# Moving VectorE's weight sums, two output sums and the index tables in a four-layer kernel

## The chip, the cores and the metric

The kernel runs on one core of one Trainium2 chip. The metric is the device time of one execution in microseconds (us). TensorE (PE) multiplies matrices, VectorE (DVE) and GpSimd (POOL) do elementwise work, ScalarE (ACT) does activations, and SyncE (SP) issues most of the transfers. Each engine takes its own instructions strictly in the order in which the program lists them; between engines, semaphores order the work.

## The reference, cut to what matters

Eight sequences of 128 tokens, 512 wide, in float32, pass four residual layers; each layer is a "cond" and an "ffn" part:

```python
x = x + L0_ffn(L0_cond(x))   # SwiGLU with per-sequence adapters; then a routed adapter layer
x = x + L1_ffn(L1_cond(x))   # adapters; routed adapters
x = x + L2_ffn(L2_cond(x))   # attention with a paged cache; soft routing
x = x + L3_ffn(L3_cond(x))   # routed adapters; 64 gated ranks

# L0_cond, per sequence b with adapter ids[b]:
g = x @ W_gate.T + adapter(x);  u = x @ W_up.T + adapter(x)      # 1376 wide
y = (silu(g) * u) @ W_down.T + adapter(...)

# L2_cond, 32 query heads on 8 key heads of 128, cache of 512 positions:
q, k, v = x @ Wq.T, x @ Wk.T, x @ Wv.T
q, k = rope(rmsnorm(q)), rope(rmsnorm(k))
k_all, v_all = [k_cache[block_table], k], [v_cache[block_table], v]
o = softmax(mask(q @ k_all.T / sqrt(128))) @ v_all
y = o @ Wo.T
```

The integer inputs are small tables: the adapter of each sequence for layers 0 and 1, its cache length, the pages of its cache and a language number for layer 3.

## The kernel before, in words

**Products with seven multiplications.** Projections, output products, gates and down products are computed as 2x2 blocks with seven block products in place of eight (Strassen, in Winograd's form). The left operand gives sums s1 to s4, the right one sums t1 to t4. `seven` (L956) writes one such product. Its PE order is: `one` = a11 b11; `p6` = s2 t2; `p5` = s1 t1; `six` = s3 t3; then a12 b21 onto `one`, s4 b22 onto `p5`, a22 t4 onto `six`. Two running sums u1 (L983: p6 plus `one`) and u2 (L985: p5 plus u1) are made by VectorE, and `six` plus u2 is written out (c22) before a22 t4 may be added onto the same bank; likewise u2 must have read `p5` before s4 b22 is added onto it. The argument `at` is a dictionary of hooks: whatever stands under "u1", "u2", "c22", "c12", "six" and so on is put into the program at that place.

**Attention in 32 steps.** A step n is a pair (qd, p): one of 8 key heads with its 4 query heads, and one of 4 pairs of sequences. I call the steps with p = 0, 1, 2, 3 the first to fourth of a head. In the loop of `run` (from L1307) step n does, in PE's order: scores of its first sequence (`weigh`, tile st, L1134), the projection q, k, v of step n + 1 (`project`: q_one, q_six, q_five, L970), the output product of step n - 1 (`leave`: wo_one, wo_two, wo_six, L970), scores of its second sequence, the first product with the values (`mix`, av, L1185), column sums (`summed`), the second product with the values.

VectorE's part of a step, in its order: four additions of the exponentials of the first sequence (`added`, part, L1154), the division of the output of step n - 1 (`divided`, oT, L1195, which waits for the reciprocals R that SP copies to other partitions), and then inside the projection's hooks u1, u2, the four left sums of the output product (`outputs`, os, L929), the blocks of q, k, v (L1019: first q and vals from `six`, then q and vals from `five`, then q and k from `six`), the rotation's straight products (r, L1064), the output product's u1 and u2, its block y (L1215), the rest of the rotation and its turn (qkt, L1111), the additions of the second sequence, the reciprocals of the sums (rr, L1170).

**The right sums of the weights** (`blocks.factors`, L877) are VectorE's too, four generators' steps per head: for the projection weights (tile q_s, 128x768 elements each) t1 and t2 are made at the end of a third step, t3 behind the first addition of the fourth step (L1313) and t4 in the hook "u2" of the projection there, behind the four left sums; for the output weights (tile o_s, 128x512 each) t1, t2 and t3 are made in the hook "c22" of the projection of a second step, and t4 in the hook "c22" of its output product. The first head's output weights are made in step 1, where the turn of a gathered cache block (kt, L1095) stands in the same hook.

**Shared order.** Once `running` is filled, nearly every instruction goes through `kept`, which holds it to the order of the program on its engine. POOL computes the rotation's crossed products (vq, vk, L1059) as soon as q and k are written, and issues the gathers of cached keys and values (L913).

**The start.** Layer 0's gates come in 11 slices of 128 columns (f = 0 to 10). Slice 0 is multiplied plainly; at its end the adapter products are masked by VectorE (tgm, tum, L369) and added. From slice 1 on `gates_by_seven` (L432) is used; per slice VectorE does u, p, p for each half of the tokens (L456, L457, L459) and, at the end, ten operations of L474 to L479. The loop (L541) also deals out the steps of the angle tables, three behind each slice from f = 2 on. Before that, the small integer tables are loaded by SP and turned into floats and row numbers by VectorE (`ints`, L130; mask1, kvrow L191, bias3): 3 casts, 1 mask, 2 x 11 operations for the cache rows and 2 for the bias. They have no fixed place in VectorE's queue; the scheduler put them between slice 0's operations.

```python
def some(ops, k=1):
    return lambda: [next(ops, None) for _ in range(k)]
...
    sums_of, outs = added(n, 0), iter(())
    next(sums_of)
    some(w_ops)()
    if n:
        divided(n - 1)
        outs = outputs(n - 1)
```

Of the kernel before, what the change touches and what calls it, by code (L numbers as in the profile page):

```python
# [10 lines left out]
F32 = mybir.dt.float32  # L11
I32 = mybir.dt.int32
AF = mybir.ActivationFunctionType
ALU = mybir.AluOpType
# [33 lines left out]
def forward(ctx: ExitStack, tc: tile.TileContext, a: dict, out: bass.AP):  # L48
# [81 lines left out]
    def ints(name, n, where=const):  # L130
        ti = where.tile([P, n], I32, tag=name + "_i", name=name + "_i")
        sp.dma_start(ti, a[name].partition_broadcast(P))
        tf = where.tile([P, n], F32, tag=name, name=name)
        dve.tensor_copy(tf, ti)
        return tf
# [27 lines left out]
        ALU.is_lt,  # L163
    )

    ids1 = ints("adapter_ids", NB)
    lens = ints("seqlens", NB)
    lang = ints("lang_ids", NB)
    table = ints("block_table", NB * 16, w0)


    mask1 = const.tile([P, NB], F32, tag="mask1", name="mask1")
    dve.tensor_scalar(mask1, ids1, p_div16, None, ALU.is_equal)

    kvrow = {}
    for what, order in (("v", "p (b c j) -> p b c j"), ("k", "p (b j c) -> p b c j")):
        selp = w0.tile([P, NB, 4, 4], F32, tag="selp", name="selp_" + what)
        dve.tensor_tensor(  # L180
            selp,
            table.rearrange(order, b=NB, c=4),
            block32.unsqueeze(1).unsqueeze(1).to_broadcast([P, NB, 4, 4]),
            ALU.mult,
        )
        page = const.tile([P, NB * 4], F32, tag="page", name="page_" + what)
        dve.tensor_reduce(page.rearrange("p (b c) -> p b c", c=4), selp, AX.X, ALU.add)
        dve.tensor_scalar(page, page, 32.0, p_mod32, ALU.mult, ALU.add)
        kvrow[what] = const.tile([P, NQ, NB * 4], I32, tag="kvrow_" + what, name="kvrow_" + what)
        for qd in range(NQ):  # L190
            dve.tensor_scalar(kvrow[what][:, qd, :], page, float(NQ), float(qd), ALU.mult, ALU.add)  # L191


    bias3 = const.tile([P, NB, 8], F32, tag="bias3", name="bias3")
    dve.tensor_tensor(
        bias3,
        eight.unsqueeze(1).to_broadcast([P, NB, 8]),
        lang.unsqueeze(2).to_broadcast([P, NB, 8]),
        ALU.is_equal,
    )  # L200
    dve.tensor_scalar(bias3, bias3, 5.0, None, ALU.mult)


    def load_small(dst_pool, name, shape, src, tag=None, bufs=None):
        kw = {} if bufs is None else {"bufs": bufs}
# [112 lines left out]
    with c0:  # L318
# [219 lines left out]
        banks = gates(0, first, lora_in)  # L538
        lora_gates(0, banks)
        rot, angles, turn_angles = rotary(tc, rp, w0, lens, part, rows, kept)  # L540
        for f in range(1, NF):  # L541
            after = f + 1 < NF and weight_sums(f + 1, gate_weights(f + 1))
            gates_by_seven(f, A)
            A = after
            if f == 2:
                down_loaded()
            for i in itertools.islice(angles, 3 * (f > 1)):
                kept(i)
            if f == NF // 2:
                AW = [down_weights(0, wop.tile([P, 3, NH, P], F32, tag="os", name="wds_0"))]  # L550
# [241 lines left out]
def attention(tc, a, x, ident, lens, kvrow, part, ww, wop, ypool, sums, rot, eps, psa, c2, chunks, mm):  # L792
# [106 lines left out]
    def every(ops):  # L899
        for _ in ops:  # L900
            pass
# [136 lines left out]
    def squares(n, m, j, heads):  # L1038

        for i in heads:  # L1040
            sq = wk.tile([P, HD], F32, tag="sq", name=f"sq{m}_{n}_{j}_{i}", bufs=1)
            col = i if m == "q" else REP
            kept(act.activation(sq, S[n][m][:, j, i, :], AF.Square, accum_out=S[n]["ssq"][:, j, col : col + 1]))  # L1043
# [104 lines left out]
    def added(n, j):  # L1148

        t, u = (wk.tile([P, REP * P], F32, tag=f"part{k}{j * (k == 0)}", name=f"part{k}_{n}_{j}", bufs=1) for k in range(2))  # L1150
        c = [S[n]["pT", j][:, k, :, :].rearrange("p i t -> p (i t)") for k in range(NC)]
        S[n]["part", j] = t
        for o, l, r in ((t, c[0], c[1]), (u, c[2], c[3]), (t, t, u), (t, t, c[4])):
            kept(dve.tensor_tensor(o, l, r, ALU.add))  # L1154
            yield
# [125 lines left out]
    def run(pool_, end_of, bank, keep):  # L1281
        late.append(pool_)
        y2 = ypool.tile([P, NB, D], F32, tag="y", name="y2")
        Y.append(y2)
        pool.memset(y2, 0.0)

        idle = psa.tile([P, 512], F32, tag="mm", name="idle_q", bufs=3)
        for _ in range(3):
            kept(pe.matmul(idle, x[:, 0, 0:P], x[:, 0, 0:512], start=True, stop=True))
        for j in range(2):  # L1290
            squares(1, "q", j, range(REP))
            squares(1, "k", j, (0,))
        keys_terms = rotate(1)
        read_cached = turn_cached(1, "xs")
        keys_terms()
        gather(1, "v")
        roots(1)
        rotated(1)
        normed(1)
        turn(1)  # L1300
        end, prepared = None, iter(())
        w_ops, wo_ops = iter(()), WO[0].factors()

        def some(ops, k=1):
            return lambda: [next(ops, None) for _ in range(k)]

        for n, (qd, p) in enumerate(steps):  # L1307

            after = n + 1 if 0 < n < len(steps) - 1 else None
            weigh(n, 0)  # L1310
            sums_of, outs = added(n, 0), iter(())
            next(sums_of)
            some(w_ops)()  # L1313
            if n:
                divided(n - 1)
                outs = outputs(n - 1)
                if not after:
                    every(outs)
            every(sums_of)
            if after:  # L1320
                project(after, {
                    "u2": lambda: (every(outs), every(w_ops)),
                    "c22": lambda: (turn_cached(2)() if n == 1 else None, some(wo_ops, 3)()),
                    "c11": lambda: (squares(after, "k", 0, (0,)), squares(after, "q", 0, (0, 1))),
                    "c12": lambda: squares(after, "q", 0, (2, 3)),
                })
                keys_terms = rotate(after)
                if n + 2 < len(steps):
                    if steps[n + 2][1] == 0:
                        weights(steps[n + 2][0])  # L1330
                    gather(n + 2, "k")
                leave(n - 1, {
                    "one": lambda: (
                        squares(after, "q", 1, range(REP)), squares(after, "k", 1, (0,)), roots(after),
                    ),
                    "c22": lambda: (every(wo_ops), keys_terms(), rotated(after), normed(after), turn(after)),
                })
                fetch(after)
                gather(after, "v")
            if n + 2 == len(steps):  # L1340
                end.load_w2()
                end.load_aw()
            mixed = mix(n, 0)
            left = (lambda: leave(n - 1),) if n and not after else ()
            weigh(n, 1, {2: (some(mixed), *left), 3: (some(mixed),), 4: (some(mixed, NC),)})
            if left:
                end.shifted()
            sums_of = added(n, 1)
            if n == 0:
                some(sums_of, 2)()  # L1350
                fetch(1, read_cached)
                gather(2, "k")
            every(sums_of)
            if 0 < n < len(steps) - 2 and steps[n + 2][1] == 0:
                w_ops = W[steps[n + 2][0]].factors()
                some(w_ops, 2)()
            summed(n)
            inverted(n)
            if n == 0:
                every(tokens(2))  # L1360
            if n == 5:
                prepared = end.prepare(bank, lambda shape, name: wk.tile(shape, F32, tag="xs", name=name, bufs=1))
            next(prepared, None)
            every(mix(n, 1))
            next(prepared, None)
            if n and p == 0:
                out_weights(qd)
                wo_ops = WO[qd].factors()
            if 0 < n < len(steps) - 2:
                turn_cached(n + 2)()  # L1370
                every(tokens(n + 2))
            if n == 3:
                kept(keep())
            if n == 4:
                end = end_of(kept)

            if qd == NQ - 1 and p:
                for j in range(2):
                    end.turn(y2, 2 * (p - 1) + j, bank)
            if n + 2 == len(steps):  # L1380
                end.low(0, bank)
                end.anchors(0, bank)
        divided(n)
        every(outputs(n))
        end.product(0, "st", bank)
        leave(n)
        return y2, end
# [903 lines left out]
```

## Time and profile before

| what | value |
|---|---|
| median of 3 runs | 1540.5 us (1537.6 to 1541.04) |
| the profiled execution's own time | 1540.52 us |
| its span from first to last instruction | 1538.6 us |
| granted clock of TensorE | 0.999 |
| PE busy in the span | 1510.6 us (98%) |
| DVE / POOL / ACT busy | 1048.7 / 843.9 / 543.9 us |
| PE busy from 345 to 1360 us (attention) | 1004.55 of 1015 us |
| PE busy from 0 to 170 us (gates) | 165.11 of 170 us |

A row of the timeline reads: start in us, duration in us, engine, line, operation, output<-inputs, shape, count, and in brackets the idle time of the engine just before it with what ended it. A row of the list of waits reads: who waited <- for whom: total us, how often, the longest. A row of the chain (the work that ended last, followed back) has start, duration and engine. Matmul rows come two to a float32 matmul, and their ends overlap the next row's start by some 0.16 us.

### The profile page before, as it was taken

To read this page: it belongs to the slowest core of one execution; us is meant where nothing else is said; L and a number is where in the kernel's file an instruction comes from. 1 tells how busy PE (TensorE), PEld (TensorE's weight loads), DVE (VectorE), ACT (ScalarE), POOL (GpSimd) and SP (SyncE) were. 2 spreads that over 40 slices of the span, in tenths; PEclk is the share of its full clock that TensorE was granted. 3 is DMA by queue.
4 is the path that set the end of the run, shared out by engine and by line. 5 is a ranking of instruction groups with operands and counts; after the bars stand their busy time and mean duration, and the time that the engine had idled before them with its cause. 6 is when DMAs were issued, how large, how long until landed. Compare 5 with 4: busy or idle time off the path is not lost.

```text
span 1538.6 us, 19053 instructions
## 1 busy us (share of the span) xinstructions
PE 1510.6 (98%) x6127; PEld 947.0 (62%) x6127; DVE 1048.7 (68%) x2057; ACT 543.9 (35%) x1336; POOL 843.9 (55%) x870
## 2 busy tenths in 40 slices
PE   9999999999999999999999999999999999999998
PEld 7888886444555555555555555555555556559886
DVE  4666435477877786777777677777867878755375
ACT  1111110144444444444444444445434445431110
POOL 2241105285766777676677767667777767531210
PEclk9999999999999999999999999999999999999999
DMA  7311001153655544564444445444445534332001
GB/s 234 115 42 31 1 0 62 53 146 96 176 146 151 142 110 123 141 175 115 127 143 117 123 136 171 117 128 144 122 123 141 166 110 127 101 111 92 1 9 50
DMA packets 157837, 169.92 MB, mean 110 GB/s; under 512 B 54272, under 2 KB 129216, under 8 KB 157600
## 3 DMA queue, kind: packets, MB, share of 16 engines
q1 hardware_dynamic: 139296, 131.27, 30.7%
q0 software_dynamic: 17056, 36.49, 8.0%
q8 instruction: 51, 0.84, 0.2%
q10 hardware_dynamic: 1376, 0.85, 0.2%
q14 instruction: 58, 0.48, 0.1%
HBM read 113.89 MB, written 42.07 MB: 101 GB/s over the span
## 4 chain that ended last, share of the span: by engine, by line
PE 88%; DVE 7%; DMA 3%; issue 1%; ACT 0%; POOL 0%; SPq 0%; ACTq 0%; DVEq 0%
PE st L1134 17%; PE av L1185 17%; PE g L362 8%; PE q_six L970 7%; PE wo_two L970 5%; PE dn L362 5%; PE q_five L970 4%; PE q_one L970 4%; PE wo_one L970 3%; PE wo_six L970 3%; PE eo_l L53 2%; PE h L1719 2%; PE z L1719 2%; PE o L1719 1%; PE midp_l L53 1%
## 5 line engine op out<-in xcount | busy, mean ns | idle before, releaser
L913 POOL DMA_INDIRECT kn<-in_k_cache,kvrow_k x256 | 279.8, 1093 | 73.3 <-issue 69.4
L913 POOL DMA_INDIRECT vals<-in_v_cache,kvrow_v x256 | 261.6, 1022 | 73.4 <-issue 62.6
L1185 PE MATMUL av<-pT,vals 128*128 128x512 f32 x640 | 298.8, 597 | 0.0
L1138 ACT ACTIVATE pT<-st,hide 128x512 f32<-128x512 f32 x256 | 175.9, 687 | 318.5 <-PE st L1134 194.4
L1134 PE MATMUL st<-qT,kT 128*128 128x512 f32 x512 | 236.4, 594 | 2.8 <-DMA qT<-turned_new 2.2
L1059 POOL TENSOR_TENSOR vq<-q,txq 128x256 f32<-128x256 f32 x128 | 120.3, 967 | 181.4 <-DVE q L1019 102.4
L1185 PEld LDWEIGHTS av<-pT,vals 128*128 128x128 f32 x640 | 118.9, 190 | 144.0 <-issue 142.1
L1134 PEld LDWEIGHTS st<-qT,kT 128*128 128x128 f32 x512 | 96.5, 190 | 112.9 <-issue 106.4
L1154 DVE TENSOR_TENSOR part<-pT 128x512 f32<-128x512 f32 x128 | 87.1, 687 | 64.7 <-issue 44.2
L1170 DVE RECIPROCAL rr<-sum 128x256 f32<-128x256 f32 x32 | 56.2, 1758 | 73.0 <-PE av L1185 37.8
L970 PE MATMUL q_one<-q,x 128*128 128x384 f32 x256 | 93.0, 486 | 0.0
L1043 ACT ACTIVATE sqq<-q 128x128 f32<-128x128 f32 x256 | 79.4, 310 | 22.9 <-DVE q L1019 15.9
L970 PEld LDWEIGHTS q_one<-q,x 128*128 128x128 f32 x256 | 48.5, 190 | 39.8 <-issue 14.4
L970 PE MATMUL q_six<-q_s,xs_all 128*128 128x384 f32 x192 | 69.8, 486 | 0.0
L1134 PE MATMUL st<-qT,kTn 128*128 128x512 f32 x128 | 65.5, 593 | 1.0 <-ACT pT L1138 1.0
L970 PE MATMUL wo_one<-o,oT 128*128 128x256 f32 x256 | 65.7, 379 | 0.0
L1024 ACT COPY q<-q_one 128x256 f32<-128x256 f32 x32 | 11.9, 372 | 145.9 <-PE q_one L970 145.9
L970 PE MATMUL wo_two<-o_s,os 128*128 128x256 f32 x256 | 60.8, 380 | 1.7 <-DVE vals L1019 1.3
L1138 ACT ACTIVATE pT<-st,rs 128x512 f32<-128x512 f32 x64 | 44.0, 687 | 38.3 <-PE av L1185 20.6
L970 PEld LDWEIGHTS wo_one<-o,oT 128*128 128x128 f32 x256 | 48.6, 190 | 13.4 <-PE st L1134 0.2
L429 POOL TENSOR_TENSOR ws<-wu 128x256 f32<-128x256 f32 (+1 forms) x9 | 6.4, 712 | 91.3 <-DMA wu<-in_WuT 82.4
L362 PE MATMUL g<-xs,ws 128*128 128x256 f32 (+1 forms) x240 | 55.1, 379 | 0.0
(450 smaller groups left out, 2796.5 us busy)
## 6 DMA issues: line engine op xcount, KB each, us to landing
turned_new<-qkt SPq DMA_DIRECT2D x126, 160.0 KB
turned_cached<-kt SPq DMA_DIRECT2D x128, 128.0 KB
kT<-turned_cached SPq DMA_DIRECT2D x32, 512.0 KB
qT<-turned_new SPq DMA_DIRECT2D x32, 512.0 KB
R<-R SPq DMA_DIRECT2D x96, 128.0 KB
q<-in_WqT SPq DMA_DIRECT2D x8, 1024.0 KB
o<-in_WoT SPq DMA_DIRECT2D x8, 1024.0 KB
kn<-in_k_cache,kvrow_k POOLq DMA_INDIRECT x256
```

What stands on the lines that cost most here:

```text
L53: pe.matmul(o, lhsT, rhs, start=start, stop=stop)
L362: pe.matmul(o, lhsT, rhs, start=start, stop=stop, skip_group_check=True)
L913: kept(pool.indirect_dma_start(out=d[:, c, :], out_offset=None, in_=kc if what == "k" else vc, in_offset=bass.IndirectOffsetOnAxis(ap=kvro ...
L970: kept(pe.matmul(o, l[:, c, :], r[:, c, :], start=start and c == 0, stop=c == 1, skip_group_check=True))
L1043: kept(act.activation(sq, S[n][m][:, j, i, :], AF.Square, accum_out=S[n]["ssq"][:, j, col : col + 1]))
L1059: kept(pool.tensor_tensor(to, t[:, b, :, hi : hi + 64], wx[:, b, lo : lo + 64].unsqueeze(2).to_broadcast(list(to.shape)), ALU.mult,))
L1134: kept(pe.matmul(ps, s["kT"][:, c, 4 * j : 4 * j + 4, :] if c < 4 else s["kn"][:, j], s["qT"][:, :, REP * j : REP * (j + 1), :].rearrange( ...
L1138: kept(act.activation(pT[:, c, :, :].rearrange("p i t -> p (i t)"), ps, AF.Exp, **(dict(bias=hide[:, b, c : c + 1]) if c < 4 else dict(bia ...
L1154: kept(dve.tensor_tensor(o, l, r, ALU.add))
L1170: kept(dve.reciprocal(r, S[n]["sum"]))
L1185: kept(pe.matmul(ps, v[:, c, :], pT[:, c, :, :].rearrange("p i t -> p (i t)"), start=c == 0, stop=c == NC - 1, skip_group_check=True,))
L1719: return pe.matmul(o, lhsT, rhs, start=start, stop=stop, skip_group_check=True)
```

## The change

Five things move; nothing is added to or removed from the work of the attention or the tables.

1. **Projection weights.** t3 and t4 of the next head's projection weights are both made at the start of the fourth step, ahead of the first addition. Before, t3 came behind that addition and t4 in the hook "u2".
2. **Output sums.** Two of the four left sums of the output product (os) go from behind u2 to between u1 and u2 of the projection (hook "u1"), in all steps 1 to 30.
3. **Output weights.** In a second step, t1 and t2 go from hook "c22" to hook "c12" of the projection, behind the q and vals of `five`; t3 goes to a hook "six" of the output product, which puts it behind the rotation's straight product and ahead of that product's u1; t4 stays.
4. **Step 1's turn of a cache block** goes along to hook "c12", behind t1 and t2.
5. **Tables.** The adapter, language and page tables are made by a generator; its 28 operations are dealt five to a slice of the gates behind the angle steps, from f = 3 on. Their three loads stand later in SP's queue, behind the norms' loads and ahead of the third slice's weights. The cache lengths stay where they were.

PE's, ACT's and POOL's instructions keep their order.

```diff
-    ids1 = ints("adapter_ids", NB)
     lens = ints("seqlens", NB)
-    lang = ints("lang_ids", NB)
-    table = ints("block_table", NB * 16, w0)
...
+    def tables():
+        read = {}
+        for name, n, where in (
+            ("adapter_ids", NB, const), ("lang_ids", NB, const), ("block_table", NB * 16, w0),
+        ):
+            ti = where.tile([P, n], I32, tag=name + "_i", name=name + "_i")
+            sp.dma_start(ti, a[name].partition_broadcast(P))
+            read[name] = ti, where.tile([P, n], F32, tag=name, name=name)
+        for ti, tf in read.values():
+            yield dve.tensor_copy(tf, ti)
...
+        yield dve.tensor_scalar(mask1, ids1, p_div16, None, ALU.is_equal)
...
         rot, angles, turn_angles = rotary(tc, rp, w0, lens, part, rows, kept)
+        tabled = tables()
         for f in range(1, NF):
...
-            for i in itertools.islice(angles, 3 * (f > 1)):
+            for i in itertools.chain(itertools.islice(angles, 3 * (f > 1)), itertools.islice(tabled, 5 * (f > 2))):
                 kept(i)
...
             sums_of, outs = added(n, 0), iter(())
+            if n:
+                some(w_ops, 2)()
             next(sums_of)
-            some(w_ops)()
             if n:
                 divided(n - 1)
                 outs = outputs(n - 1)
...
                 project(after, {
-                    "u2": lambda: (every(outs), every(w_ops)),
-                    "c22": lambda: (turn_cached(2)() if n == 1 else None, some(wo_ops, 3)()),
+                    "u1": some(outs, 2),
+                    "u2": lambda: every(outs),
                     "c11": lambda: (squares(after, "k", 0, (0,)), squares(after, "q", 0, (0, 1))),
-                    "c12": lambda: squares(after, "q", 0, (2, 3)),
+                    "c12": lambda: (
+                        squares(after, "q", 0, (2, 3)), some(wo_ops, 2)(), turn_cached(2)() if n == 1 else None,
+                    ),
                 })
...
+                    "six": some(wo_ops),
                     "c22": lambda: (every(wo_ops), keys_terms(), rotated(after), normed(after), turn(after)),
```

More of the change, by code (lines that the diff above doesn't have):

```diff
@@ L164, in forward @@
     )
-    ids1 = ints("adapter_ids", NB)
     lens = ints("seqlens", NB)
-    lang = ints("lang_ids", NB)
-    table = ints("block_table", NB * 16, w0)
     mask1 = const.tile([P, NB], F32, tag="mask1", name="mask1")
[L173 to L184, printed above, removed]
-        )
[L186 to L191, printed above, removed]
@@ L194, in forward @@
[L194 to L201, printed above, removed]
+    kvrow = {w: const.tile([P, NQ, NB * 4], I32, tag="kvrow_" + w, name="kvrow_" + w) for w in "vk"}
+    bias3 = const.tile([P, NB, 8], F32, tag="bias3", name="bias3")
+    def tables():
[8 more added lines that the diff above has]
+            yield dve.tensor_copy(tf, ti)
+        ids1, lang, table = (tf for _, tf in read.values())
+        yield dve.tensor_scalar(mask1, ids1, p_div16, None, ALU.is_equal)
+        for what, order in (("v", "p (b c j) -> p b c j"), ("k", "p (b j c) -> p b c j")):
+            selp = w0.tile([P, NB, 4, 4], F32, tag="selp", name="selp_" + what)
+            yield dve.tensor_tensor(
+                selp,
+                table.rearrange(order, b=NB, c=4),
+                block32.unsqueeze(1).unsqueeze(1).to_broadcast([P, NB, 4, 4]),
+                ALU.mult,
+            )
+            page = const.tile([P, NB * 4], F32, tag="page", name="page_" + what)
+            yield dve.tensor_reduce(page.rearrange("p (b c) -> p b c", c=4), selp, AX.X, ALU.add)
+            yield dve.tensor_scalar(page, page, 32.0, p_mod32, ALU.mult, ALU.add)
+            for qd in range(NQ):
+                yield dve.tensor_scalar(kvrow[what][:, qd, :], page, float(NQ), float(qd), ALU.mult, ALU.add)
+        yield dve.tensor_tensor(
+            bias3,
+            eight.unsqueeze(1).to_broadcast([P, NB, 8]),
+            lang.unsqueeze(2).to_broadcast([P, NB, 8]),
+            ALU.is_equal,
+        )
+        yield dve.tensor_scalar(bias3, bias3, 5.0, None, ALU.mult)
```

## The prediction, made blind

> **What bounds the kernel now.** I read the page's totals, then PE's waits, then the chain, then the timelines of single steps.
>
> ```profile
> PE 1510.6 (98%) x6127; PEld 947.0 (62%) x6127; DVE 1048.7 (68%) x2057; ACT 543.9 (35%) x1336; POOL 843.9 (55%) x870
> ```
> ```profile
> PE q_six L970 <- DVE vals L1019: 5.3, 10, 0.8
> PE st L1134 <- DMA qT<-turned_new: 2.2, 3, 1.6
> PE gu L362 <- DVE tgm L369: 1.8, 1, 1.8
> ...
> PE g L362 <- DVE p L457: 1.2, 2, 0.9
> ```
>
> PE is the bound: 1510.6 of 1538.63 us. PE's own work does not change, so the change can only move its gaps, 20.8 us in sum with 7.3 us of tail. The list says which are DVE's. To see what the list rounds away I measured, in every attention step, the stretch from the projection's first q_one to the next step's first st. The shortest, in step 8, is 590.09 to 605.16 = 15.07 us; the excess over it sums to 0.7 us in the first steps of the heads, 4.2 in the second, 4.5 in the third and 5.45 in the fourth. Below, a "place" is the time after the step's first q_one.
>
> **Fourth steps: a gain.** Step 15 starts its projection at 824.22.
>
> ```profile
> 822.57 0.69 DVE L1154 TENSOR_TENSOR part<-pT 128x512 f32<-128x512 f32 x1 [2.12 <-issue]
> ...
> 831.37 0.95 DVE L877 TENSOR_TENSOR q_s<-q,q_s 128x768 f32<-128x768 f32 x1
> 832.24 0.42 DVE L1019 TENSOR_TENSOR q<-q_six,uq 128x256 f32<-128x256 f32 x1
> 832.58 0.28 DVE L1019 TENSOR_TENSOR vals<-q_six,uq 128x128 f32<-128x128 f32 x1
> ```
> ```profile
> 832.91 0.91 PE L970 MATMUL q_six<-q_s,x 128*128 128x384 f32 x2 [0.79 <-DVE vals L1019]
> ```
>
> t4 (0.95, a pitch of 0.87) stands ahead of the q and vals that PE waits for, and the gap is 0.79: without it vals is in time. DVE idles 2.12 us before the first addition; t3 and t4 (0.87 each) fit there. Five of the seven fourth steps have about 1.9 to 2.15 idle there; steps 3 and 27 have only 0.43, so t4 delays their additions by some 1.3, but t3 leaves the additions' far side and the 1.5 us that u2 waits for q_five (829.44) takes most of it up. I take the whole excess: **-5.45**. Ends: -5.75 (the matmul overlap, 0.16, regained in two steps more) and 0 (PE's signals are late and vals was not what came last).
>
> **Third and first steps.** u2 needs u1's result, so the pitch between them is 0.65 for an instruction of 0.55 (step 2: u1 at place 4.60, u2 at 5.25); two os between them fill the 0.1 that is lost there and again behind u2. So u2 ends 1.8 behind u1's start in place of 1.2, and the q and vals that PE waits for end 3.0 behind it in place of 3.2. PE's s4 b22 (due at 6.45) now waits for u2 where u1 starts after place 4.6, hardly in step 2 and by 1.0 to 1.2 in steps 6 and 18, whose u1 comes at 5.6 and 5.8; these were late by about as much through vals before. Recomputed for each of the eight third steps, their excess goes from 4.5 to 3.04: **-1.4**; first steps, with the same 0.2: **-0.6** of 0.7. Ends together +1 (every later u2 counts in full) and -3 (0.2 earlier vals in all).
>
> **Second steps: a loss.** Step 9 starts its projection at 623.10.
>
> ```profile
> 630.09 0.68 DVE L877 TENSOR_TENSOR o_s<-o 128x512 f32<-128x512 f32 x1
> 630.80 0.69 DVE L877 TENSOR_TENSOR o_s<-o,o_s 128x512 f32<-128x512 f32 x1
> 631.41 0.69 DVE L877 TENSOR_TENSOR o_s<-o 128x512 f32<-128x512 f32 x1
> 632.02 0.42 DVE L1019 TENSOR_TENSOR q<-q_five,uq 128x256 f32<-128x256 f32 x1
> ...
> 633.08 1.35 DVE L1064 TENSOR_TENSOR r<-q,tsq 128x1024 f32<-128x1024 f32 x1
> ```
> ```profile
> 634.72 1.03 PE L970 MATMUL wo_six<-o_s,os 128*128 128x256 f32 x4
> ```
> ```profile
> 632.61 3.77 POOL L1059 TENSOR_TENSOR vq<-q,txq 128x256 f32<-128x256 f32 x4 [6.30 <-DVE q L1019]
> ```
>
> Before, three sums fill the time from place 6.99 (630.09) in which DVE would wait for q_five (final at 7.90, when PE's s4 b22 ends), and wo_six starts at 11.62 (634.72) without waiting. After, DVE idles from 6.99 to 7.94, and t1 to t3 come behind: q and vals 7.94 to 8.5, t1 to 9.16, t2, the two writes from `six`, r, then t3. With DVE alone, pitches 0.54 + 0.68 + 0.61 + 0.53 + 1.2 + 0.7 put t3's end near 12.3, 0.7 past 11.62. But POOL's four vq start 0.17 behind q (632.44 to 632.61), so at about 8.53, just when t1 runs, and they slow DVE's instructions that read SBUF twice, and are slowed:
>
> ```profile
> 868.27 1.77 DVE L1064 TENSOR_TENSOR r<-q,tsq 128x1024 f32<-128x1024 f32 x1
> ```
> ```profile
> 308.81 1.24 DVE L1064 TENSOR_TENSOR r<-q,tsq 128x1024 f32<-128x1024 f32 x1
> 309.98 0.94 DVE L1064 TENSOR_TENSOR r<-k,tsk 128x256 f32<-128x256 f32 x1
> ```
>
> The same r takes 1.24 or 1.77, and the small one 0.94 here against 0.41 at 871.52 with POOL idle; o_s rows range from 0.68 to 1.0. DVE and POOL seem to take turns, instruction by instruction. Dealt so, with 0.6 for a vq by itself (3.77 for four, less r's 1.26 in step 8): t1 to 9.16, vq to 9.75, t2 to 10.30, vq to 10.89, r to 11.97, vq to 12.56, t3 to 13.11. Then wo_six starts at 13.17 in place of 11.62: 1.6 late. The displacement also makes wo_two (s2 t2, due 9.89) 0.4 to 0.5 late, which is within that 1.6. Five ordinary second steps at 1.65 make 8.25; step 13 has 1.8 and step 5 1.97 (both start late), and step 1 about 3.6, because the cached block's two transposes (0.71 + 0.66) stand between t2 and the rest. Sum 15.6 against 4.2: **+11.5**. Ends: +4.5 (no turns: 0.8 in each, 2.6 in step 1) and +20 (POOL's first vq beats t1: wo_six at 14.4, 2.8 each).
>
> [...]
>
> **The copies of q.** Two of the three waits of st for DMA qT, 0.30 and 0.23 shown, follow second steps (9 and 25). There DVE's t4 and rest come 0.6 earlier relative to PE's later stream, so the copies start earlier: **-1.07** (each gap, some 0.25 of lost overlap and pickup included). Ends 0 and -1.1.
>
> **The head of the kernel.**
>
> ```profile
> 8.03 13.26 DMA adapter_ids_i<-in_adapter_ids
> ```
> ```profile
> 90.34 1.10 PE L362 MATMUL g<-x,ws 128*128 128x256 f32 x4 [0.89 <-DVE p L457]
> ```
>
> The tables land at 21.28, and DVE converts them until tgm at 26.43, which needs none of them (its masks come from another table) and only stands behind them; PE gets tgm's product at 26.90 after 1.83 of idling. After, tgm can run near 23.6, when PE's adapter product t is done (23.15), and PE goes from its former gu row to it at 25.08. Gain 26.90 - 25.08 and the overlap: **-2.05**. Ends: 0 (the cache lengths, whose table stays ahead, land later than now) and -2.1.
>
> The 28 operations return in slices 4 to 8, in front of the next slice's u, p, p. They take 0.63, 0.85, 0.44, 0.98 and 0.44 us there. Slices 5 and 7 wait for p already (0.89 at 90.34, 0.28 at 117.59), so all of theirs counts, 0.85 + 0.98; slice 4 has 0.52 of slack (+0.19), 6 has 0.44 (+0.05), 8 has 0.85 (0). **+2.07**; ends +0.5 (half of it runs while DVE waits anyway) and +3.3 (all of it). POOL's and SP's queues: the three loads pass behind two norm loads and ahead of slice 2's weights, 85 us before the first gather needs a row; nothing.
>
> **Sum.** -5.45 - 1.44 - 0.6 - 1.07 - 2.05 + 2.07 + 11.5 = **+3.0 us**, on 1540.52 of the profiled execution, which is the median (1540.5): 1543.5 us. 0.2% is 3.1 us, about what a measurement of this kernel can tell from no change.
>
> **Rivals.**
> - *A* (0.50), the forecast: t1 gets ahead of vq and turns are taken. 1543.5, with 1540 to 1547 by the single terms; half of it over +3.1.
> - *B* (0.25): POOL comes first, in half or all of the second steps. For it: q is written 0.05 before t1 can start, and in the row 868.27 0.03 of lateness was enough. Second steps +16 to +20: 1548 to 1552.
> - *C* (0.20), the other side: no turns. [...] It decides from a t3 that ends before place 12.9, where the second steps' loss equals the other gains (8.5). For it: POOL has been asleep for 6.3 us before vq, and o_s rows of 0.68 are the most frequent.
> - *D* (0.05): the change does not do what it says. vals is not what PE waited for in fourth steps, and the 5.45 stay: 1549.
>
> **How the numbers follow.** Slower by over 0.2%: 0.26 of A, B, D: 0.56. Faster: nearly all of C and a little of A: 0.19. The rest 0.25. The range from C's middle to B's nearer half: 1536.5 to 1550.
>
> **What would show it.** Right: in fourth steps no gap of q_six by vals; in second steps wo_six waiting for o_s some 1.5 us, vq rows of four over 4.2 us, o_s rows near 1.2; PE's gap by tgm gone from 26 us; slices 5 and 7 waiting 0.8 to 1 us more. Wrong: wo_six at place 11.6 to 12.4 (C), at 14 and later (B), or fourth steps still 15.8 us long (D).

## The result, and the profile after

The changed kernel took 1551.82 us in the median of 17 runs (1547.63 to 1556.99), the kernel before 1540.5 us (17 runs, 1535.37 to 1549.35): a ratio of 1.0065, 95% interval 1.005 to 1.0081, so 8 to 12 us slower. The forecast was 1543.5 us with a range to 1550. The profiled execution had a span of 1553.3 us against 1538.6 (+14.7), and that is split below.

First the page's line of busy times and the waits of PE, after:

```profile
PE 1516.9 (98%) x6127; PEld 952.8 (61%) x6127; DVE 1049.7 (68%) x2057; ACT 544.7 (35%) x1336; POOL 848.9 (55%) x870
```
```profile
PE wo_six L979 <- DVE o_s L886: 8.4, 8, 2.6
PE g L370 <- DVE p L465: 6.9, 2, 5.3
PE st L1143 <- ACT pT L1147: 4.4, 1, 4.4
PE wo_two L979 <- DVE o_s L886: 3.1, 8, 0.4
```

Two things are to be seen. q_six no longer waits for vals (5.3 us before), and wo_six and wo_two now wait for the output weights in all eight second steps, as forecast. But PE's busy time has grown by 6.3 us with the same 6127 rows, and there is a single wait of 5.3 us among the gates. Both were not forecast.

The busy time first. The windows over the gates (us from the start, then width, PE busy, PEld, DVE, ACT, POOL, and after them the granted clock):

```profile
92.00:94.00 2.00, 0.72 (x2) 0.66 (x3) 1.85 (x5) 0.00 (x0) 0.31 (x1) 0.64 0.00 0
94.00:96.00 2.00, 2.00 (x7) 1.55 (x6) 0.85 (x2) 0.00 (x0) 0.00 (x0) 0.50 0.00 0
96.00:98.00 2.00, 2.00 (x6) 1.64 (x5) 0.00 (x0) 0.00 (x0) 0.00 (x0) 0.50 0.00 0
```

From 92.56 on PE's clock was granted at half for 6.83 us. It was so again for 6.83 us at 358.8 and for 3.41 us at 379.3; before, it was so only in the last microseconds (from 1534.45).

Now the wait of 5.3 us. VectorE, GpSimd and PE in slice 5, after:

```profile
87.84 0.27 DVE L198 TENSOR_REDUCE page_v<-selp_v 128x32 f32<-128x128 f32 x1
88.15 1.20 DVE L199 TENSOR_SCALAR page_v<-page_v,within 128x32 f32<-128x32 f32 x1
89.38 2.97 DVE L201 TENSOR_SCALAR kvrow_v<-page_v 128x32 int32<-128x32 f32 x3
```
```profile
87.72 1.59 POOL L528 TENSOR_TENSOR wds<-wds,wd 128x640 f32<-128x640 f32 x1
89.27 1.53 POOL L528 TENSOR_TENSOR wd<-wd 128x640 f32<-128x640 f32 x1
90.76 1.55 POOL L528 TENSOR_TENSOR wds<-wd,wds 128x640 f32<-128x640 f32 x1
```
```profile
93.28 2.04 PE L370 MATMUL g<-x,ws 128*128 128x256 f32 x4 [5.30 <-DVE p L465]
```

The five table operations of slice 5 end at 92.35, 4.5 us after they began. The reduction takes its 0.27 us. page_v ends at 89.35, right behind a sum of GpSimd (89.31), and the last kvrow at 92.35, right behind another (92.31). One by one the three kvrow take 1.45, 0.17 and 1.51 us, about a microsecond each in the mean, for 32 elements. At the kernel's start, before the change, page_v took 0.24 and eight kvrow 0.78:

```profile
23.90 0.24 DVE L188 TENSOR_SCALAR page_v<-page_v,within 128x32 f32<-128x32 f32 x1
24.33 0.78 DVE L191 TENSOR_SCALAR kvrow_v<-page_v 128x32 int32<-128x32 f32 x8
```

The difference is GpSimd, which is forming the sums of the down weights just then (1.53 to 1.98 us each) and had no row between 20 and 27 us before the change; the run sums_later below tests that. PE waits for the p that stands behind them.

And a second step, step 9 of after (its projection starts at 637.88):

```profile
645.82 0.42 DVE L1028 TENSOR_TENSOR q<-q_five,uq 128x256 f32<-128x256 f32 x1 [1.82 <-PE q_five L979]
...
646.36 0.68 DVE L886 TENSOR_TENSOR o_s<-o 128x512 f32<-128x512 f32 x1
647.07 1.10 DVE L886 TENSOR_TENSOR o_s<-o,o_s 128x512 f32<-128x512 f32 x1
...
649.76 1.21 DVE L886 TENSOR_TENSOR o_s<-o 128x512 f32<-128x512 f32 x1
```
```profile
646.41 5.15 POOL L1068 TENSOR_TENSOR vq<-q,txq 128x256 f32<-128x256 f32 x4 [5.36 <-ACT sqq L1052]
```
```profile
651.12 1.10 PE L979 MATMUL wo_six<-o_s,os 128*128 128x256 f32 x4 [0.84 <-DVE o_s L886]
```

The three o_s rows are t1, t2 and t3. t1 starts 0.05 ahead of the first vq and takes 0.68; t2 takes 1.10 and t3 1.21; four vq take 5.15 where they took 3.77. wo_six starts at place 13.24 (forecast 13.17, before 11.62).

The whole difference of the two profiled spans, in us, by stretches that have the same work, with the prediction's term:

| stretch | before | after | difference | forecast |
|---|---|---|---|---|
| start to the first gate product of sums (first row g<-xs,ws) | 28.95 | 27.21 | -1.74 | -2.05 |
| from there to the first row of the adapter's down product (td) | 141.26 | 150.45 | +9.19 | +2.07 |
| down products, adapters, first projection | 138.28 | 138.28 | 0 | 0 |
| projection of step 1 to that of the next (first scores of step 1) | 42.76 | 47.21 | +4.45 | 0 |
| second steps' excess over 15.07 | 4.16 | 18.60 | +14.44 | +11.5 |
| fourth steps' excess | 5.45 | 0.00 | -5.45 | -5.45 |
| third steps' excess | 4.48 | 0.84 | -3.64 | -1.4 |
| first steps' excess | 0.68 | 0.38 | -0.30 | -0.6 |
| rest of attention, by subtraction (forecast: copies of q) | | | -0.63 | -1.07 |
| from the last projection to the end | 212.26 | 210.61 | -1.65 | 0 |
| sum | | | +14.67 | +3.0 |

### The profile page after: what moved, and what is told of

It reads as the page before. It is cut to its first block, busy times and chain, and to the rows that moved or that the text cites. A ratio compares the mean times of both kernels' runs of the same rounds, so it can differ in the third digit from the quotient of the medians.

```text
span 1553.3 us, 19053 instructions
## 1 busy us (share of the span) xinstructions
PE 1516.9 (98%) x6127; PEld 952.8 (61%) x6127; DVE 1049.7 (68%) x2057; ACT 544.7 (35%) x1336; POOL 848.9 (55%) x870
## 4 chain that ended last, share of the span: by engine, by line
PE 90%; DVE 6%; issue 1%; another core or an unknown queue 1%; ACT 0%; POOL 0%; DMA 0%; SPq 0%; DVEq 0%; ACTq 0%
PE st L1143 17%; PE av L1194 17%; PE g L370 8%; PE q_six L979 7%; PE q_five L979 5%; PE q_one L979 5%; PE dn L370 5%; PE wo_two L979 4%; PE wo_six L979 4%; PE wo_one L979 3%; PE eo_l L53 2%; PE h L1732 2%; PE z L1732 2%; DVE o_s L886 1%; PE o L1732 1%
## 5 line engine op out<-in xcount | busy, mean ns | idle before, releaser
L1068 POOL TENSOR_TENSOR vq<-q,txq 128x256 f32<-128x256 f32 x128 | 130.2, 1047 | 186.1 <-ACT sqq L1052 134.4
L1147 ACT ACTIVATE pT<-st,rs 128x512 f32<-128x512 f32 x64 | 44.0, 687 | 40.0 <-PE av L1194 20.6
L979 PEld LDWEIGHTS wo_two<-o_s,os 128*128 128x128 f32 x256 | 47.9, 190 | 12.2 <-PE wo_one L979 6.1
```

The source lines that it names most:

```text
L979: kept(pe.matmul(o, l[:, c, :], r[:, c, :], start=start and c == 0, stop=c == 1, skip_group_check=True))
L1068: kept(pool.tensor_tensor(to, t[:, b, :, hi : hi + 64], wx[:, b, lo : lo + 64].unsqueeze(2).to_broadcast(list(to.shape)), ALU.mult,))
L1147: kept(act.activation(pT[:, c, :, :].rearrange("p i t -> p (i t)"), ps, AF.Exp, **(dict(bias=hide[:, b, c : c + 1]) if c < 4 else dict(bia ...
```

## The experiments

Times of one set are compared on one chip, with runs of the kernel before beside them. "Excess" is, as in the prediction, what a step needs over 15.07 us from its first q_one to the next st.

### First set: the parts taken apart

**tables_back**: the changed kernel, its tables as before.

```diff
+    ids1 = ints("adapter_ids", NB)
     lens = ints("seqlens", NB)
+    lang = ints("lang_ids", NB)
+    table = ints("block_table", NB * 16, w0)
...
-            for i in itertools.chain(itertools.islice(angles, 3 * (f > 1)), itertools.islice(tabled, 5 * (f > 2))):
+            for i in itertools.islice(angles, 3 * (f > 1)):
```

> The changed kernel with the tables loaded and converted at the start, as before; the weight sums and output sums stay moved. Theory 1 (of the 12.8 us between the two profiled executions, some 7.4 arise ahead of attention: three row operations of VectorE each wait for a weight sum of GpSimd of 1.5 us, TensorE idles 5.3 us and then runs 6.8 us at half its clock): the first q_one of attention comes near 299 us as before, no halved clock in the gates, and the time is 7 us under the changed kernel, about 5 us (0.35%) over the kernel before. Theory 2 (the tables cost the 2 us that the prediction took, the 5.3 us were a chance of that one execution): about 10 us (0.65%) over the kernel before, and a halved clock shows up elsewhere.

Measured: 1539.35 against 1532.15 us, ratio 1.0058 (1.0041 to 1.0075), so +9 us by the ratio. The gates' stretch is 140.91 us, with no halved clock there. The halved clock and the 5.3 us belong to the tables, as theory 1 has it. The time is above its +5 all the same. That number was taken off the 12.8 us between two profiled executions, and the one of before had a high excess in its attention (14.8 us; 9.1 in tables_only, which has the same order there); this may be the reason, but no run of before was profiled on this chip.

**outw_back**: the changed kernel, the output weights' sums and step 1's turn of a cache block as before.

```diff
-                    "c12": lambda: (
-                        squares(after, "q", 0, (2, 3)), some(wo_ops, 2)(), turn_cached(2)() if n == 1 else None,
-                    ),
+                    "c22": lambda: (turn_cached(2)() if n == 1 else None, some(wo_ops, 3)()),
+                    "c12": lambda: squares(after, "q", 0, (2, 3)),
...
-                    "six": some(wo_ops),
```

> The changed kernel with the output weights' sums (and the cached block's turn in step 1) where they were before; tables, projection weights and output sums stay moved. Theory 1 (all the loss in attention is in the eight second steps, some 14 us plus the wait and halved clock of step 1): wo_six never waits for o_s, and the time is about 2 us under the kernel before (-0.1%, with the gates still 7.4 late and the third and fourth steps 10 us better). Theory 2 (the gains of the third and fourth steps come from the later place of the output weights, the loss from elsewhere): third and fourth steps lose again and the time is at or above that of the changed kernel, +10 us.

Measured: 1532.23 against 1532.15, ratio 0.9996 (0.998 to 1.0012). Second steps' excess 2.14 us, third 0.32, fourth 0; no wait for o_s. Theory 2 falls. Slice 5 waits 5.31 us here too, and 6.83 us at half the clock follow.

**both_back**: both of these, so that only the projection weights and the two output sums are moved.

> Only the projection weights and the two output sums are moved; tables and output weights as before. Theory 1 (parts add up): third, fourth and first steps lie at 15.07 us from q_one to st, second steps as before, and the time is 8 to 10 us under the kernel before (-0.6%). Theory 2 (what VectorE gains in fourth steps is given back in the second steps of the next head or in the copies of q): within 3 us of the kernel before.

Measured: 1523.55 against 1532.15, ratio 0.9956 (0.9939 to 0.9974): 4 to 9 us faster. Excess: second steps 1.65, third 1.41, first and fourth 0. Theory 1.

**tables_only**: the kernel before, with the tables alone dealt among the gates.

> The kernel before with the tables alone loaded later and dealt among the gates. [...] Theory 2 (the prediction: 2.05 us gained at tgm, 2.07 lost in slices): 0, within 1.5 us.

Measured: 1539.49 against 1532.15, ratio 1.0063 (1.0046 to 1.0081). Its gates' stretch is 148.79 us, slice 5 waits 5.32. Theory 2, the prediction's zero for the tables, is refuted.

### Second set: why the tables are slow

**after_again**: the changed kernel on the chip of this set.

> The changed kernel itself, beside the kernel before on the chip of this set. Theory 1 (parts add up: -8.6 for the weight and output sums, +8.7 for the tables, +15.8 for the output weights, each measured in the first set): about +14 to +16 us over the kernel before. Theory 2 (the second steps' delay and the late tables share a cost, so that the +10 of the result holds on any chip): +10.

Measured: 1552.5 against 1540.36, ratio 1.0084 (1.0059 to 1.0109): 9 to 17 us, which holds both theories' numbers. Inconclusive between them; that the kernel is slower by about 0.7% is repeated.

**sums_later**: outw_back with GpSimd's down sums at slice 9, where only the last three table operations stand.

```diff
-            if f == NF // 2:
+            if f == 9:
                 AW = [down_weights(0, ...)]
```

> Weight sums, output sums and tables moved as in the change, output weights as before, and GpSimd's four sums of the down weights at slice 9 in place of slice 5, where no table operation stands. Theory 1 (the row operations are slow because each waits for one of GpSimd's sums): kvrow rows take 0.1 us each, slice 5 waits 1.5 to 2 us in place of 5.3, the clock is not halved there, 5 to 7 us under the kernel before. Theory 2 (they are slow by themselves in that place): slice 5 still waits 5 us and the time is that of the kernel before.

Measured: 1532.53 against 1540.36, ratio 0.9955 (0.9935 to 0.9975). Slice 5 of this kernel:

```profile
87.06 0.35 DVE L201 TENSOR_SCALAR kvrow_v<-page_v 128x32 int32<-128x32 f32 x3
```
```profile
88.35 1.10 PE L370 MATMUL g<-x,ws 128*128 128x256 f32 x4 [0.52 <-DVE p L465]
```

The same three kvrow take 0.35 us, not 2.97, in the same place of VectorE's queue; PE waits 0.52 us, its clock stays whole, and the gates' stretch is 143.57 us. The operations are slow only beside GpSimd's sums. Even r_sin's last operation, ahead of them, takes 0.43; in slice 5 of before it was

```profile
87.76 1.65 DVE L1425 TENSOR_SCALAR r_sin<-r_sin 128x512 f32<-128x512 f32 x1
```

Of the 2.3 us by which this stretch is longer than in before (141.26), most is in slice 7, where PE waits 1.52 us (before 0.28), and in slice 9, where it waits 0.75: there one of the last table operations stands beside the moved sums and takes 1.42 us.

**warm**: outw_back with ten matmuls without use ahead of the product that waits in slice 5. They write into the unused half of the tile of `one`, and slice 5's gates are not the reference's.

```diff
                 into(one[:, 0], a12, b21, False)
+                if f == 5 and one is B[0][0]:
+                    for _ in range(10):
+                        kept(pe.matmul(one[:, 1], a12[:, 0, :], b21[:, 0, :], start=True, stop=True, ...))
                 into(two[:, 1], s4, b22, False)
```

> Weight sums, output sums and tables moved as in the change, output weights as before, and ten matmuls without use in slice 5, ahead of the product that waits (their result is not read). Theory 1 (the clock is halved because TensorE has idled 5.3 us): the gap shrinks to 1 us, no halved clock near 92 us, and with the same end of VectorE's work the time is 2 to 3 us under the same kernel without them, so 2 to 3 us under the kernel before. Theory 2 (the halving has another cause): the clock halves there all the same and the time is that of the kernel before.

Measured: 1537.24 against 1540.36, ratio 0.9984 (0.9969 to 0.9999). PE and the windows of this kernel:

```profile
93.30 1.10 PE L370 MATMUL g<-x,ws 128*128 128x256 f32 x4 [1.02 <-DVE p L465]
```
```profile
94.00:96.00 2.00, 2.00 (x11) 1.74 (x10) 0.86 (x3) 0.00 (x0) 0.00 (x0) 1.00 0.00 0
```

The product starts at 93.30, as in after (93.28), since VectorE is as late. But its four rows take 1.10 us and not 2.04, and the window from 94 to 96 is at full clock. The gates' stretch is 146.96 us against 150.08 in outw_back: 3.1 us were the clock, which was halved behind 5.31 us of idle time and stayed whole behind 1.02. The gain in time fits (some 2 us between the two ratios, on different chips), though the intervals alone would not show it.

**idle_tables**: tables late, dealt five to a slice, but into VectorE's idle time behind the last u, p, p of a slice; output weights as before.

```diff
                 B.append((one, two, six, p1, u, b21, b22, t4))
+            for i in between:
+                kept(i)
             for one, two, six, _, _, b21, b22, t4 in B:
```

> Weight sums and output sums moved, output weights as before, tables loaded late, but dealt five to a slice into VectorE's idle time, behind the last u, p, p of a slice and ahead of its end. Theory 1 (the tables cost only because they stand with GpSimd's sums in front of a waiting TensorE): no gap over 1 us at slices 5 and 7, no halved clock in the gates; 9 to 10.5 us under the kernel before. Theory 2 (any table operation dealt among the gates delays them): 3 to 5 us under it.

Measured: 1530.42 against 1540.36, ratio 0.9935 (0.9912 to 0.9958): 6 to 14 us faster than the kernel before, and 22 us faster than the changed kernel in the same set (which also has the output weights' move). Gates' stretch 141.40 us, as without any tables in it. Theory 1. The operations that were slow in after now come one slice earlier, in slice 4, where GpSimd forms no sums; in slice 5 five others stand beside the sums:

```profile
75.97 0.24 DVE L199 TENSOR_SCALAR page_v<-page_v,within 128x32 f32<-128x32 f32 x1
76.24 0.35 DVE L201 TENSOR_SCALAR kvrow_v<-page_v 128x32 int32<-128x32 f32 x3
```
```profile
90.50 2.07 DVE L201 TENSOR_SCALAR kvrow_v<-page_v 128x32 int32<-128x32 f32 x5
94.53 0.42 DVE L484 TENSOR_TENSOR up<-g,u 128x256 f32<-128x256 f32 x1 [1.96 <-PE g L370]
```

These five still wait for GpSimd (2.07 us), but VectorE is idle for 1.96 us behind them, so nothing waits for them. Whether the late tables make this kernel faster than both_back, whose tables stay at the start, the two intervals do not tell.

### Third set: the second steps, and each move alone

**no_cross**: tables_back with GpSimd's vq left out in second steps.

```diff
+            if after and p == 1:
+                S[after]["zero"] = zero = wk.tile([P, 2, REP, HD], F32, tag="vq", ...)
+                kept(pool.memset(zero, 0.0))
...
-            for b in (...):
+            for b in () if zero else (...):
```

> The changed kernel with the tables as before, and in second steps GpSimd's four crossed products of q (vq) left out: their place is filled with zeros before the projection, so these steps' q is not the reference's. [...] Theory 2 (the order of VectorE's queue alone makes the delay): o_s rows as with vq, 1.7 each, +7.

Measured: 1532.33 against 1531.42, ratio 0.9998 (0.9981 to 1.0014). The same step's t2 and its wo_six:

```profile
626.84 0.69 DVE L877 TENSOR_TENSOR o_s<-o,o_s 128x512 f32<-128x512 f32 x1
```
```profile
630.21 1.10 PE L970 MATMUL wo_six<-o_s,os 128*128 128x256 f32 x4 [0.56 <-DVE o_s L877]
```

t2 takes 0.69 and not 1.10, t3 0.94 (vk is still there), and an ordinary second step's excess is 1.02 in place of 1.70. So 0.7 of the 1.7 us is due to GpSimd's vq. The other 1.0 is the order of VectorE's queue together with vk, beside which t3 takes 0.25 more than t2. The turns with vq and the order of the queue (theory 2) each hold a part; which is the larger, this run leaves open.

**t3_early**: tables_back with t3 directly behind t1 and t2.

```diff
-                        squares(after, "q", 0, (2, 3)), some(wo_ops, 2)(), ...
+                        squares(after, "q", 0, (2, 3)), some(wo_ops, 3)(), ...
-                    "six": some(wo_ops),
```

> The changed kernel with the tables as before, and t3 of the output weights directly behind t1 and t2, ahead of the last q and k of the projection and of r. Theory 1 (PE waits for t3 because r and two vq stand before it): wo_six is 0.4 late through wo_two alone, but r, u1, u2, y and t4 come 0.6 later and the last wo_six waits for t4; the second steps' excess is 1.2 in place of 1.7, +3 to +4 us over the kernel before. Theory 2 (what counts is that three sums stand behind q_five's values at all): 1.7 as before, +7.

Measured: 1535.41 against 1531.42, ratio 1.0024 (1.0005 to 1.0043). By the time this is theory 1; by the trace it is nearly theory 2. An ordinary second step's excess is 1.56: wo_six no longer waits for t3, but in its place the next wo_two waits 0.36 for u2 of the output product, which comes later by the same sum. The delay moves along the queue and does not go; the order of before, with the sums ahead of q_five's values, where VectorE idles, had no such wait.

**proj_only** and **os_only**: the kernel before with one move each.

> The kernel before with the projection weights' t3 and t4 alone moved. By the prediction the fourth steps gain 5.45 and the others nothing: -5.5 us. If the two output sums carry part of the -8.6 that both gave together, this is -5 to -6 and the rest is theirs; if they carry nothing, -8.6.

> The kernel before with the two output sums alone moved. By the prediction third steps gain 1.4 and first steps 0.6: -2 us; in fourth steps t4 still stands ahead of vals, and their 5.5 us of waiting stay. If the sums' place is worth more than the prediction took, -3 to -4.

Measured against 1531.42 us: proj_only 1530.36, ratio 0.9991 (0.9973 to 1.001); os_only 1524.94, ratio 0.9953 (0.9935 to 0.9971). In the traces both have lost the fourth steps' excess: 0.08 and 0.95 us (before 5.45). So the two output sums, which I had given nothing in fourth steps, take PE's wait there away almost alone, although t4 still stands ahead of vals: two os less in that stretch are 0.7 us, and the gaps that fourth steps had were 0.54 to 0.79. The time of os_only, 4 to 10 us less, is beyond what I expected (-2, or -3 to -4). The time of proj_only does not show what its trace shows, which the last set was for.

### Fourth set: do the two moves overlap

> Projection weights alone moved, on one chip with the two kernels it is compared with. Theory 1 (in fourth steps either move alone takes vals off PE's way, since the gap was 0.44 to 0.79 us and each move gives 0.7 to 0.9, so the two overlap): -4 to -6 us against the kernel before. Theory 2 (the first set's -1.1 is right and this move is worth next to nothing): -2 to 0.

> The two output sums alone moved. Theory 1 (overlap): -6 to -7 us, most of what both give. Theory 2: -2, as the prediction took them, and -6.5 was a chance of the executions.

> Both moved. Theory 1 (overlap): -8 to -9, clearly less than -5 and -6.5 added. Theory 2 (parts add up): the sum of the two lone results of this set.

> Both and the output weights moved, tables as before: the output weights' own cost is the difference to the kernel with both. Theory 1 (eight second steps by 14 us, and a halved clock of 1.7 behind step 1 in most executions): +15 between the two. Theory 2 (as between the changed kernel and the one with the output weights put back): +10 to +12.

These are the kernels proj_only, os_only, both_back and tables_back again, on one chip. Measured against 1534.76 us:

| kernel | median | ratio (interval) | excess in the trace |
|---|---|---|---|
| projection weights alone | 1528.06 | 0.9939 (0.9919 to 0.9959) | 4.4 |
| two output sums alone | 1524.91 | 0.9927 (0.9906 to 0.9948) | 4.9 |
| both | 1526.56 | 0.9942 (0.9917 to 0.9967) | 4.0 |
| both, and output weights | 1537.34 | 1.002 (1.0001 to 1.0039) | 16.4 |

The three upper kernels cannot be told apart: within the intervals, each move alone gives what both give. By the ratios the single moves gave 9.4 and 11.2 us, which would add up to 20.6, and both gave 8.9 (5 to 13). So they overlap, more than theory 1 had it; theory 2 is refuted for proj_pair, os_pair and both_pair. The output weights cost 12.4 us in excess between the two lowest rows, and 11 to 12 us in time, nearer to theory 2's number; in the first set it was 15.8. I take 11 to 16 us for it. That proj_only gave -1.4 on its chip (interval -4.1 to +1.5) and -9.4 here (-12.4 to -6.3) is more than the intervals allow; what differs between the two chips no run here tells, so the first is left as it stands and the size of a single move is not known better than that.

## Why the prediction was wrong, step by step

**What failed: the gates' term, "+2.07; ends +0.5 and +3.3".** It measured +9.19 in the trace. The step that failed is "They take 0.63, 0.85, 0.44, 0.98 and 0.44 us there": these durations came from rows at the kernel's start, where GpSimd was not forming sums, and were carried into slices where it is. I let VectorE and GpSimd take turns in the second steps, with the right rows, and did not ask what GpSimd runs in slice 5. I also let the turns slow only operations that read SBUF twice; page_v and kvrow read one SBUF tensor and were slowed all the same (1.20 us for page_v, 2.97 for three kvrow; 0.24 and 0.35 in sums_later). r_sin's 1.65 us in slice 5 of before (0.43 without GpSimd), one source too, was the sign of both. Slice 5's operations took 4.5 us and not 0.85, 3.7 more than priced. On that came 3.1 us of halved clock, which no term had, because the trace of before shows no idle time of PE over 1.83 us there, and slice 7 waited 0.35 us more than its term. Together that is the 7.1 us between +2.07 and +9.19; with +9.19 in its place the prediction's sum would be +10.1, inside the measured 8 to 12. What is left to the 14.7 of the two profiles is about the first scores' 4.45; the errors of the other terms cancel. Without tables the gates' stretch was 140.9 to 141.3 us in the eleven profiled kernels that have none there; with them, as dealt in the change, 148.8 to 150.5 in four.

**The head: right in the trace, and partly luck.** -1.74 for -2.05. But the eleven kernels with the tables at the start reached the same point between 26.2 and 29.1 us, 27.8 in the mean, and the seven with late tables between 26.3 and 27.5, 27.1 in the mean. The profile of before was near the slow end, so the gain is more like 0.8 us.

**Second steps: right in mechanism, too small by 3.** An ordinary one cost 1.70 for 1.65, and turns are taken as worked out (rows above). The turns were my estimate from r's 1.24 and 1.77 us; the runs show t2 at 1.10 us beside vq and at 0.69 without it (no_cross). Step 1 was 6.31 and not 3.6. The 3.6 itself was sized right: tables_back, with the same wait of 2.57 us there and no halved clock, has 3.67. In after, the halved clock behind the first scores still ran for the first 2.5 us of this step, and another 3.41 us of it came with the wait, together some 2.9 us (after_again 5.70, outw_pair 4.20). And the 4.2 us of before that the new excess replaces were a high draw, which makes the measured difference smaller: with the output weights in their old place the eleven other executions had 1.6 to 3.8.

**Fourth steps: right as a sum (-5.45) and in what PE waited for; the other half was missed.** Rival D is refuted, vals was what PE waited for, and the projection weights' move alone takes the excess to 0.08 (proj_only). But os_only shows that the output sums alone nearly do it too (0.95), so in the change the first move adds little that can be measured. The size had luck in it: with the order of before, tables_only had 3.82 and not 5.45.

**Third and first steps:** -3.94 for -2.0, past the far end given (-3). With the order unchanged (tables_only) third steps' excess was 2.4 and not 4.5, so a part of it is chance.

**First scores of step 1: not forecast, and by the runs hardly the change's.** They waited 4.4 us in the profiled execution of after and 2.5 in that of after_again, the same kernel; 3.0 in both_back and 1.0 in both_pair, again one kernel; 0.5 to 2.5 in most others and not at all in four. In before and tables_only ACT started pT there about 2.1 us apart, each on a signal of PE; in after the first pT started 5 us behind its product and the next ones 0.7 us apart. I have not found what makes ACT late; it stays open.

**The rivals.** The time fell at rival B's, for another cause: in all eight second steps t1 starts ahead of the first vq (0.05 us in step 9). Rival C (no turns, which with the second steps' low end of +4.5 gives -4.0 us and 1536.5) is refuted by t2's 1.10 us. The rival I lacked was a second place for the mechanism of the first.

## What to carry to other kernels

An operation's duration belongs to its place: before it is moved, list what the other engines run there, and price it with rows from that place; here a VectorE operation of 32 elements took 0.1 us alone and 1 us beside GpSimd's sums. Where an engine has idle time in a step, put the moved work into that idle time: here the tables behind the last u, p, p of a slice cost the gates nothing, five of them beside GpSimd's sums, and at the slices' ends they cost 8 to 9.5 us, or 2.3 with the sums moved away from slice 5. And where two moves each remove one cause of the same wait, price them together: either alone gave, as far as could be measured, what both gave.

## What the runs showed of the hardware

**Half a clock after idle time.** In all five places where PE idled 5.3 us (slice 5 of after, after_again, outw_back and tables_only) or 4.4 us (step 1 of after), its clock was at 0.500 for 3.41 or 6.83 us from about then. After 3.0 us (both_back) it was so for 3.41 us; after 2.57 us it was so for 3.41 us in after and not in tables_back; it was so once behind 0.9 and 1.7 us close together (step 1 of after_again), and after the 1.6 to 1.9 us that precede step 0's scores in none of eighteen profiled executions (1.64 in before, 1.87 in after). For slice 5 the pair outw_back and warm shows that it is the idling: with 5.31 us of it the clock was at half for 6.83 us, with 1.02 us it was at 1.00 from 92 to 100 us. The time from the start of the idling to the half clock was 4.59 us (87.97 to 92.56), 3.65 (355.15 to 358.80) and 2.49 (376.79 to 379.28) in after. In seven of the eighteen executions, before and after not among them, the clock also halved for 3.41 or 6.83 us near the end of attention, behind waits of no more than 0.9 us; no run here explains that.

**VectorE beside GpSimd.** In slice 5 of after, VectorE's operations with one SBUF source and SBUF output took longer beside GpSimd's sums of the down weights than in sums_later, where these come in slice 9: page_v 1.20 us for 0.24, three kvrow 2.97 for 0.35 (one of them 1.51), r_sin's last 1.65 for 0.43. Those with two SBUF sources were slowed beside vq in step 9 (t2 1.10 us, and 0.69 in no_cross without vq; t3 1.21). The reduction (0.27 us in slice 5 of after, 0.28 in sums_later) and the operations with a source in PSUM (u and p beside a sum in slice 5 of before, 0.41 and 0.42; q beside vq in step 9 of after, 0.41) were not.

**Spread between executions.** Executions of the kernel before spread over 14.0 us in the 17 runs of the result and over 14.6 in 18 runs of the fourth set, and a profile is one draw: the attention order of before had an excess of 14.8 us in its profile and 9.1 in that of tables_only.
